# Deformable sampling on one Trainium2 core: one broad weighting per tap, half the transposes, and a corner multiplied on GpSimd

## The chip, the cores and the metric

The kernel runs on one core of one Trainium2 chip, as one program. The metric is the device time of one execution in microseconds. Five engines of the core appear below: PE (TensorE: matmuls and transposes; its weight loads are listed as PEld), DVE (VectorE), ACT (ScalarE), POOL (GpSimd, which also issues the indirect transfers) and SP (SyncE, which issues plain transfers). SBUF is the large on-chip memory, PSUM the small one into which PE writes. All engines run their own instructions in order and wait for each other by semaphores.

## The reference

Two layers of a network over x of shape (2, 128, 64, 64). The part that matters is the first mixer: four branches of deformable convolutions with kernels of 1, 1, 3 and 7, so 1 + 1 + 9 + 49 = 60 taps in all. For each tap and each of the 4096 pixels of an image, a position (py, px) is computed, the image is sampled there bilinearly, and the sample, times a mask, goes into a product with the tap's weights:

```python
def bilinear_sample(x, py, px):
    y0 = jnp.floor(py)
    x0 = jnp.floor(px)
    ...
    return v00 * (1 - wy) * (1 - wx) + v01 * (1 - wy) * wx + v10 * wy * (1 - wx) + v11 * wy * wx

def deform_conv(x, off_w, off_b, mod_w, mod_b, reg_w, k, pad):
    ...
    sampled = bilinear_sample(x, py, px) * mask[:, None]
    return jnp.einsum('bckhw,ock->bohw', sampled, reg_w.reshape(O, C, k * k))
```

v00 to v11 are the four corners around the position. After that come group norms and a fusing 1x1 convolution, a mixture of 8 experts, then the second layer with a depthwise convolution, a state-space scan and a second mixture of experts. The change touches only the weighting of the four corners and what carries it to the product.

## The kernel before, in words

**The table.** For each batch a table in HBM holds, for each pixel position, one row with the 128 channels of all four corners (4 x 128 float32 values, 2 KB). Sampling 128 pixels at one tap is therefore one indirect transfer, which fetches 128 rows into 128 partitions.

**Tiles and loops.** A batch has 4096 pixels in 8 groups (NG) of 512, a group is GT = 4 tiles of 128 pixels. `sample` runs over the 60 taps of one group; `run` calls it for the 8 groups of batch 0, then of batch 1: 2 x 8 x 60 = 960 taps. One tap does this:

- POOL issues four gathers (line 711), one for each tile, into a buffer `v` of [128 pixels, 4 tiles, 4 corners, 128 channels]. The pool of `v` has six buffers (line 610). A gather needs the indices `idx` of the group, and a buffer that the tap six before has been read out of.
- DVE weights the corners. The weights `w4` are copied to PSUM every 30 taps as `pw` (line 723). Line 740 multiplies corners 0 and 1 of all four tiles in place (1024 elements for each partition). For each half of the tiles, line 745 multiplies corners 2 and 3 into a PSUM buffer `low` (512 elements), and line 746 adds `low` onto corners 0 and 1. Two partial sums for each tile are left in `v`.
- PE transposes these to [128 channels, 512 pixels] in PSUM (line 750, tile `pst`): eight transposes, where the second of a pair accumulates onto the first and so makes the last sum.
- ACT copies `pst` to SBUF as `st` (line 759).
- Two taps later, `product` (line 779) has PE multiply `st` with the tap's weights `regw` and accumulate it in `out`, in two halves of 128 output channels. At the end of a branch ACT copies `out` to `ys` and it goes to HBM.

**What runs in between.** The order on every engine is written out by hand (a manual schedule: instructions stay in the order in which the Python code issues them). At the end of each tap, `conv.step()` issues a piece of the offset convolution, which computes indices and weights of later groups (`offset_stream`, lines 351 to 417: small matmuls on PE in line 402, window copies on ACT, position arithmetic on DVE), and `rest.step()` two or three pieces of other work: in batch 0 the normalisation of batch 1 and constant matrices, in batch 1 the end of the mixer for batch 0, its experts (lines 917 to 1009, with the product of line 991 on DVE) and the convolutions of the second layer. The group's indices come from `new_group` tiles that the offset stream fills (batch 0) or from HBM by `load_group`, a group ahead (batch 1).

Of the kernel before, what the change touches and what calls it, by code (L numbers as in the profile page):

```python
# [10 lines left out]
F32 = mybir.dt.float32  # L11
I32 = mybir.dt.int32
AF = mybir.ActivationFunctionType
ALU = mybir.AluOpType
AX = mybir.AxisListType
PSUM = bass.MemoryType.PSUM
# [3 lines left out]
P = 128  # L20
B = 2
C = 128
# [3 lines left out]
GT = 4  # L26
# [7 lines left out]
NTAP = len(TAPS)  # L34
FIRST = [0, 1, 2, 11]
NO = 3 * NTAP
TW = H + 3
E0 = 8
E1 = 64
HID = 512  # L40
DS = 16
# [67 lines left out]
def transpose4(nc, ident, ps, srcs):  # L109
    for j, s in enumerate(srcs):  # L110
        nc.tensor.transpose(ps[:, j, :], s, ident)  # L111
# [73 lines left out]
class L0Conv:  # L185
# [416 lines left out]
    def run(self, build, after):  # L602

        env, tc, nc = self.env, self.env.tc, self.env.nc
        pools = lambda ctx: lambda name, bufs, **kw: ctx.enter_context(tc.tile_pool(name=name, bufs=bufs, **kw))
        with ExitStack() as ctx:
            pool = pools(ctx)
            self.rp, self.regw = pool("l0rw", 1), {}
            self.ip = pool("l0i", 2)
            self.vp = pool("l0v", 6)  # L610
            self.stp = pool("l0s", 2)
            self.pending = []
            first = ctx.enter_context(ExitStack())
            self.open_offsets(pools(first))
            for i in range(2):
                nc.vector.memset(self.padc[i], 0.0)
            psum = ctx.enter_context(ExitStack())
            right = lambda name: pools(psum)(name, 1, space=PSUM, side="right")
            self.p_f = deque([right("l0po")])
            cur = self.new_group(self.ip)  # L620
            with (
                tc.tile_pool(name="nrm", bufs=3) as sp,
                tc.tile_pool(name="nrmp", bufs=4, space=PSUM) as pp,
            ):
                xs = []
                for g in range(NG):
                    if g % GT == 0:
                        x = self.vp.tile([P, GT, 4 * C], F32, name="v")
                    xs.append(x[:, g % GT, :])
                    nc.sync.dma_start(out=xs[g], in_=env.d["x"][0, :, g * 512 : (g + 1) * 512])  # L630
                xn = self.vp.tile([P, GT, 4 * C], F32, name="v")
                self.load_weights()
                for _ in self.zero_table(0):
                    pass
                own = lambda g: xn[:, g % GT, :].rearrange("p (j c) -> p j c", c=C)
                norms = [self.norm_group(0, g, sp, pp, "nrm", x, own(g)) for g, x in enumerate(xs)]
                together(norms[:2], 2)

                stage = self.rows(0, 0)
                self.sum_weights()  # L640
                others = Side()
                others.add(mixed(norms[2:], 3))
                for _ in range(24):
                    others.step()
                offsets = self.offset_stream([(0, 0, cur)], stage)
                while others.todo:
                    next(offsets)
                    for _ in range(3):
                        others.step()
                self.load_chunk(0)  # L650
                for _ in self.norm_end(0):
                    pass
                for _ in offsets:
                    pass
            self.p_w = pool("l0pw", 1, space=PSUM)
            self.p_r = pool("l0pr", 1, space=PSUM)
            self.p_t = pool("l0pt", 2, space=PSUM)
            self.p_o = pool("l0py", 2, space=PSUM)
            self.pending = [(n, functools.partial(self.load_chunk, c)) for n, c in ((1, 1), (3, 2))]
            early = psum.enter_context(ExitStack())  # L660
            p_m = pools(early)("l0pm", 1, space=PSUM, side="right")

            def more():

                early.close()
                self.p_f.append(right("l0po2"))
                yield


            conv, rest = Side(), Side()  # L670
            self.late, self.made = deque(), [0, 0]
            rest.add(self.norm(1, p_m, "misc"), more(), build)
            ahead = {}

            def runs():
                for g in range(1, NG):
                    ahead[g] = self.new_group(self.ip)
                    yield 0, g, ahead[g]
                    yield 1, g - 1, None
                yield 1, NG - 1, None  # L680

            conv.add(self.offset_stream(runs()))
            for g in range(NG):
                self.sample(0, g, *cur, conv, rest, 2 if g else 3)
                cur = ahead.get(g + 1)
            conv.drain()
            rest.drain()
            psum.close()
            first.close()
            side = ctx.enter_context(tc.tile_pool(name="l0ps", bufs=2, space=PSUM))  # L690
            rest.add(after(0, side))
            cur = self.load_group(1, 0)
            for g in range(NG):
                nxt = self.load_group(1, g + 1) if g + 1 < NG else None
                self.sample(1, g, *cur, conv, rest, 2)
                cur = nxt
            for f in self.late:
                f()
            for _, f in self.pending:
                f()  # L700
            self.pending = []
            rest.drain()

    def sample(self, b, g, idx, w4, conv, rest, pace):

        env, nc = self.env, self.env.nc
        pw, vs = None, {}

        def gather(v, t, tiles):
            for j in tiles:  # L710
                nc.gpsimd.indirect_dma_start(  # L711
                    out=v[:, j, :],
                    out_offset=None,
                    in_=self.table[b],
                    in_offset=bass.IndirectOffsetOnAxis(ap=idx[:, j, t : t + 1], axis=0),
                )

        for br, (k, _) in enumerate(BRANCH):
            for t in range(FIRST[br], FIRST[br] + k * k):
                tw = t % HT  # L720
                if tw == 0:
                    pw = self.p_w.tile([P, GT, HT, 4], F32, name="pw")
                    nc.vector.tensor_copy(pw, w4[:, :, t : t + HT, :])

                if b == 0 and g == 0 and t == 0:
                    for i in range(6):
                        vs[i] = self.vp.tile([P, GT, 4 * C], F32, name="v")
                        gather(vs[i], i, range(0, 2))
                if t in vs:
                    v = vs.pop(t)  # L730
                    gather(v, t, range(2, GT))
                else:
                    v = self.vp.tile([P, GT, 4 * C], F32, name="v")
                    gather(v, t, range(GT))
                v4 = v.rearrange("p j (q c) -> p j q c", q=4)


                up = v4[:, :, 0:2, :]
                w = pw[:, :, tw, 0:2].unsqueeze(3).to_broadcast([P, GT, 2, C])
                nc.vector.tensor_tensor(up, up, w, ALU.mult)  # L740
                for j in range(0, GT, 2):
                    two = slice(j, j + 2)
                    low = self.p_r.tile([P, 2, 2, C], F32, name="low")
                    w = pw[:, two, tw, 2:4].unsqueeze(3).to_broadcast([P, 2, 2, C])
                    nc.vector.tensor_tensor(low, v4[:, two, 2:4, :], w, ALU.mult)  # L745
                    nc.vector.tensor_tensor(up[:, two], up[:, two], low, ALU.add)  # L746
                pt = self.p_t.tile([P, GT, P], F32, name="pst")
                for j in range(GT):
                    for q in range(2):
                        nc.tensor.matmul(  # L750
                            pt[:, j, :],
                            v4[:, j, q, :],
                            env.ident,
                            is_transpose=True,
                            start=j == 0 and q == 0,
                            stop=j == GT - 1 and q == 1,
                        )
                st = self.stp.tile([P, 512], F32, name="st", bufs=3)
                nc.scalar.copy(st, pt.rearrange("p j t -> p (j t)"))  # L759
                self.late.append(functools.partial(self.product, b, g, br, t, st))  # L760
# [799 lines left out]
class L1Ffn:  # L1560
# [8 lines left out]
    def fetch(self, pool):  # L1569

        c = len(self.w1)
        w1 = pool.tile([P, EC, HID], F32, name="wt")
        src = self.env.d["weight1"][c * EC : (c + 1) * EC, 0:C, :].rearrange("e p h -> p e h")
        self.env.nc.sync.dma_start(out=w1, in_=src)
        self.w1.append(w1)
# [329 lines left out]
```

## Time and profile before

| what | value |
|---|---|
| median of 3 runs | 7961.13 us (7953.55 to 7967.98) |
| the profiled execution's own time | 7970.23 us |
| its span, first to last instruction | 7968.4 us |
| mean granted TensorE clock | 0.832 |
| busy over the span | PE 5681.7 us (71%), DVE 5782.8 (73%), POOL 4612.1 (58%), ACT 1988.5 (25%) |
| first gather issued, last one | 108.1 us, 5808.9 us |
| 128 to 2935 us: eight groups of batch 0 | 5.8 to 5.9 us a tap for most groups |
| 2935 to 5817 us: eight groups of batch 1 | 5.5 to 6.3 us a tap |
| the rest, from 5820 us on | 2148 us |

In the rows of the profile, "L711 POOL DMA_INDIRECT v<-table,idx x3840 | 3650.0, 951 | 2123.6 <-issue" reads: line 711 on POOL, an indirect transfer that writes `v` from `table` and `idx`, 3840 times; busy for 3650.0 us, 951 ns each; the engine stood idle for 2123.6 us just before such instructions, and the most of it ended with what is named behind the arrow ("issue": nothing that the profile shows; "remote": an event that it can't place). For a gather, the busy time on POOL is the issuing of its descriptors, not the transfer. In lists in order of time the columns are the start in us, the duration in us, then engine, line and operation, and in brackets the idle time before it.

### The profile page before, as it was taken

How to read it: one execution, taken by the hardware profiler on the slowest of the kernel's cores; microseconds unless marked ns; L12 is line 12 of the kernel's file. 1: busy time of each engine (PE TensorE's matmuls, PEld its weight loads, DVE VectorE, ACT ScalarE, POOL GpSimd, SP SyncE). 2: the span in 40 equal slices, each digit the busy share in tenths (PEclk: the TensorE clock that was granted, in tenths of full speed). 3: DMA queues.
4: the chain of work that ended last, by engine and by line, in shares of the span. 5: the costliest groups of instructions: out<-in, count | busy, mean ns of one | idle time of the engine just before them, and what ended most of it. 6: DMA issues, size and time to landing. Idle time of an engine off the chain costs nothing. (4 is left out here: it accounts for less than half of the span.)

```text
span 7968.4 us, 77973 instructions
## 1 busy us (share of the span) xinstructions
PE 5681.7 (71%) x25153; PEld 3608.9 (45%) x25153; DVE 5782.8 (73%) x8700; ACT 1988.5 (25%) x3838; POOL 4612.1 (58%) x4589
## 2 busy tenths in 40 slices
PE   4677777777777767767766878765555678756668
PEld 3455555555555534434444656543333456512124
DVE  5877777777777777678787666676756575789982
ACT  1111111111111113211111222211154255455540
POOL 3666666666666666666666666566643334357640
PEclk8888888888888878878888888887787778877789
DMA  7886767677676777877777877777654334434444
GB/s 221 254 270 210 220 206 220 211 215 219 207 221 205 217 226 256 275 237 248 229 239 211 228 208 219 217 217 229 203 163 146 116 99 134 115 128 147 148 136 148
DMA packets 645247, 1597.35 MB, mean 200 GB/s; under 512 B 168020, under 2 KB 253180, under 8 KB 640876
## 3 DMA queue, kind: packets, MB, share of 16 engines
q0 software_dynamic: 307200, 1006.88, 41.6%
q1 hardware_dynamic: 306156, 537.52, 21.4%
q10 hardware_dynamic: 31488, 47.97, 1.7%
q8 instruction: 205, 3.36, 0.2%
q14 instruction: 198, 1.62, 0.1%
HBM read 1478.65 MB, written 115.83 MB: 200 GB/s over the span
## 5 line engine op out<-in xcount | busy, mean ns | idle before, releaser
L711 POOL DMA_INDIRECT v<-table,idx x3840 | 3650.0, 951 | 2123.6 <-issue 1003.8
L779 PE MATMUL out<-st,regw 128*128 128x512 f32 x3840 | 2142.1, 685 | 131.2 <-issue 79.9
L750 PE MATMUL pst<-ident,v 128*128 128x128 f32 x7680 | 1264.9, 306 | 1072.0 <-issue 662.4
L740 DVE TENSOR_TENSOR v<-v,pw 128x1024 f32<-128x1024 f32 x960 | 1168.3, 1217 | 704.2 <-DMA v<-table,idx 566.9
L750 PEld LDWEIGHTS pst<-ident,v 128*128 128x128 f32 x7680 | 1011.9, 158 | 1455.6 <-issue 985.2
L759 ACT COPY st<-pst 128x512 f32<-128x512 f32 x960 | 557.3, 585 | 4350.9 <-remote 2356.1
L746 DVE TENSOR_TENSOR v<-v,low 128x512 f32<-128x512 f32 x1920 | 1318.1, 687 | 68.0 <-remote 1.5
L745 DVE TENSOR_TENSOR low<-v,pw 128x512 f32<-128x512 f32 x1920 | 1328.7, 692 | 33.4
L1426 POOL TENSOR_TENSOR db<-du,bcb 128x512 f32<-128x512 f32 x512 | 657.3, 1289 | 835.4 <-DVE da L1477 683.7
L779 PEld LDWEIGHTS out<-st,regw 128*128 128x128 f32 x3840 | 771.5, 223 | 747.7 <-issue 684.4
L1449 PE MATMUL py<-sc,ident 128*128 128x512 f32 x1024 | 660.6, 751 | 233.0 <-DVE sc L1487 233.0
L1477 DVE TENSOR_TENSOR_SCAN da<-da,state,db 128x512 f32<-128x512 f32 x512 | 657.0, 1283 | 177.9 <-ACT da L1433 134.4
L1449 PEld LDWEIGHTS py<-sc,ident 128*128 128x128 f32 x1024 | 200.2, 229 | 529.3 <-DVE sc L1487 436.2
L402 PEld LDWEIGHTS po<-wa,win 128*128 128x128 f32 x2112 | 330.2, 202 | 141.8 <-issue 141.2
L1152 PEld LDWEIGHTS ps<-ipw,hs 128*120 128x120 f32 x2816 | 343.3, 199 | 109.1 <-issue 75.4
L1487 DVE TENSOR_TENSOR sc<-da,bcb 128x512 f32<-128x512 f32 x512 | 354.2, 692 | 44.8 <-DVE da L1477 1.8
L402 PE MATMUL po<-wa,win 128*128 128x147 f32 x2112 | 358.3, 299 | 35.2 <-issue 34.2
L1152 PE MATMUL ps<-ipw,hs 128*120 128x64 f32 x2816 | 340.8, 281 | 45.3 <-issue 30.8
L1433 ACT ACTIVATE da<-delta,w_A_log 128x512 f32<-128x512 f32 x512 | 354.0, 692 | 18.8 <-DVE delta L1389 2.8
L1160 PEld LDWEIGHTS ps<-tm,X 120*88 120x88 f32 x2048 | 188.7, 170 | 83.7 <-ACT Y L1114 53.3
L1160 PE MATMUL ps<-tm,X 120*88 120x48 f32 x2048 | 195.6, 267 | 41.9 <-ACT Y L1114 37.9
L855 PE MATMUL pfo<-yc,fw 128*128 128x256 f32 x512 | 146.9, 423 | 80.4 <-ACT yc L857 67.3
(296 smaller groups left out, 4695.2 us busy)
## 6 DMA issues: line engine op xcount, KB each, us to landing
bcb<-bc SPq DMA_DIRECT2D x256, 512.0 KB
regw<-in_regw SPq DMA_DIRECT2D x192, 640.0 KB
v<-table,idx POOLq DMA_INDIRECT x3840
yd<-ys ACTq DMA_DIRECT2D x128, 256.0 KB
yc<-yd SPq DMA_DIRECT2D x32, 1024.0 KB
gb<-gd SPq DMA_DIRECT2D x16, 2048.0 KB
wt<-in_weight SPq DMA_DIRECT2D x32, 1024.0 KB
tm<-pos SPq DMA_DIRECT2D x16, 1440.0 KB
```

The source lines that it names most:

```text
L402: m()
L711: nc.gpsimd.indirect_dma_start(out=v[:, j, :], out_offset=None, in_=self.table[b], in_offset=bass.IndirectOffsetOnAxis(ap=idx[:, j, t : t ...
L740: nc.vector.tensor_tensor(up, up, w, ALU.mult)
L745: nc.vector.tensor_tensor(low, v4[:, two, 2:4, :], w, ALU.mult)
L746: nc.vector.tensor_tensor(up[:, two], up[:, two], low, ALU.add)
L750: nc.tensor.matmul(pt[:, j, :], v4[:, j, q, :], env.ident, is_transpose=True, start=j == 0 and q == 0, stop=j == GT - 1 and q == 1,)
L759: nc.scalar.copy(st, pt.rearrange("p j t -> p (j t)"))
L779: nc.tensor.matmul(self.out[half], self.regw[t // CH][:, t % CH, half * P : (half + 1) * P], st, start=first, stop=last,)
L1152: nc.tensor.matmul(ps[:, k, :], patch, own, start=True, stop=True)
L1426: nc.gpsimd.tensor_tensor(dbs[u], pieces[k]["du"][:, half, :], bcb[u // 2][:, 0, :], ALU.mult)
L1449: nc.tensor.matmul(py[k, half], by, what, start=first, stop=last)
L1477: nc.vector.tensor_tensor_scan(s, s, dbs.pop(u), state[:, half, n : n + 1], ALU.mult, ALU.add)
```

## The change

It replaces the five DVE operations of a tap by three, and the eight transposes by four. One multiplication weights all four corners in place (2048 elements), one add puts corners 2 and 3 onto 0 and 1 (1024 elements, both operands in SBUF), one adds corner 1 onto corner 0 (512 elements, both in SBUF). PE then transposes the single sum of each tile; the PSUM buffer `low` is gone.

In every second tap (EVERY = 2; the odd ones) DVE's multiplication covers only corners 0 to 2 (1536 elements), and corner 3 is multiplied on POOL (512 elements, with the weights from `w4` in SBUF). POOL runs in order, so that its multiplication of a tap doesn't stand ahead of the next tap's gathers, gathers are issued one tap ahead: in the iteration of tap t those of tap t+1 come first and then the multiplication of tap t. Buffers that have been asked for are kept in `held`. At the last tap of a group the first gathers of the next group are issued, with the indices that `after()` returns. In the very first group the first two tiles of six taps are gathered first, as before.

```diff
+EVERY = 2
...
-            self.p_r = pool("l0pr", 1, space=PSUM)
...
+        def fetch(idx, t):
+            if t in vs:
+                v = vs.pop(t)
+                self.gather(b, v, idx, t, range(2, GT))
+            else:
+                v = new()
+                self.gather(b, v, idx, t, range(GT))
+            return v
...
+        if not self.held:
+            self.held.append(fetch(idx, 0))
...
+                if t + 1 < NTAP:
+                    self.held.append(fetch(idx, t + 1))
+                elif after():
+                    self.held.append(fetch(after()[0], 0))
+                v = self.held.popleft()
                 v4 = v.rearrange("p j (q c) -> p j q c", q=4)
-
-
+                side = t % EVERY == EVERY - 1
+                if side:
+                    w = w4[:, :, t, 3:4].to_broadcast([P, GT, C])
+                    nc.gpsimd.tensor_tensor(v4[:, :, 3, :], v4[:, :, 3, :], w, ALU.mult)
+                n = 3 if side else 4
+                w = pw[:, :, tw, 0:n].unsqueeze(3).to_broadcast([P, GT, n, C])
+                nc.vector.tensor_tensor(v4[:, :, 0:n, :], v4[:, :, 0:n, :], w, ALU.mult)
                 up = v4[:, :, 0:2, :]
-                w = pw[:, :, tw, 0:2].unsqueeze(3).to_broadcast([P, GT, 2, C])
-                nc.vector.tensor_tensor(up, up, w, ALU.mult)
-                for j in range(0, GT, 2):
-                    two = slice(j, j + 2)
-                    low = self.p_r.tile([P, 2, 2, C], F32, name="low")
-                    w = pw[:, two, tw, 2:4].unsqueeze(3).to_broadcast([P, 2, 2, C])
-                    nc.vector.tensor_tensor(low, v4[:, two, 2:4, :], w, ALU.mult)
-                    nc.vector.tensor_tensor(up[:, two], up[:, two], low, ALU.add)
+                nc.vector.tensor_tensor(up, up, v4[:, :, 2:4, :], ALU.add)
+                nc.vector.tensor_tensor(v4[:, :, 0, :], v4[:, :, 0, :], v4[:, :, 1, :], ALU.add)
                 pt = self.p_t.tile([P, GT, P], F32, name="pst")
-                for j in range(GT):
-                    for q in range(2):
-                        nc.tensor.matmul(
-                            pt[:, j, :],
-                            v4[:, j, q, :],
-                            env.ident,
-                            is_transpose=True,
-                            start=j == 0 and q == 0,
-                            stop=j == GT - 1 and q == 1,
-                        )
+                transpose4(nc, env.ident, pt, [v4[:, j, 0, :] for j in range(GT)])
```

`gather` and the loop that issues a tap's four transfers move from a local function to a method and are otherwise the same; `transpose4` (lines 109 to 111) is one transpose for each of the four tiles.

More of the change, by code (lines that the diff above doesn't have):

```diff
@@ L611, in run @@
             self.stp = pool("l0s", 2)
-            self.pending = []
+            self.pending, self.held = [], deque()
             first = ctx.enter_context(ExitStack())
@@ L683, in run @@
             for g in range(NG):
-                self.sample(0, g, *cur, conv, rest, 2 if g else 3)
+                self.sample(0, g, *cur, conv, rest, 2 if g else 3, lambda: ahead.get(g + 1))
                 cur = ahead.get(g + 1)
@@ L694, in run @@
                 nxt = self.load_group(1, g + 1) if g + 1 < NG else None
-                self.sample(1, g, *cur, conv, rest, 2)
+                self.sample(1, g, *cur, conv, rest, 2, lambda: nxt)
                 cur = nxt
@@ L702, in run, with gather, sample @@
             rest.drain()
-    def sample(self, b, g, idx, w4, conv, rest, pace):
+    def gather(self, b, v, idx, t, tiles):
+        for j in tiles:
+            self.env.nc.gpsimd.indirect_dma_start(
+                out=v[:, j, :],
+                out_offset=None,
+                in_=self.table[b],
+                in_offset=bass.IndirectOffsetOnAxis(ap=idx[:, j, t : t + 1], axis=0),
+            )
+    def sample(self, b, g, idx, w4, conv, rest, pace, after):
         env, nc = self.env, self.env.nc
         pw, vs = None, {}
[L709 to L715, printed above, removed]
-                )
+        new = lambda: self.vp.tile([P, GT, 4 * C], F32, name="v")
+        def fetch(idx, t):
[6 more added lines that the diff above has]
+            return v
+        if b == 0 and g == 0:
+            for i in range(6):
+                vs[i] = new()
+                self.gather(b, vs[i], idx, i, range(0, 2))
+        if not self.held:
+            self.held.append(fetch(idx, 0))
         for br, (k, _) in enumerate(BRANCH):
@@ L723, in sample @@
                     nc.vector.tensor_copy(pw, w4[:, :, t : t + HT, :])
[L725 to L734, printed above, removed]
@@ L747, in sample @@
-                pt = self.p_t.tile([P, GT, P], F32, name="pst")
-                for j in range(GT):
-                    for q in range(2):
-                        nc.tensor.matmul(
-                            pt[:, j, :],
-                            v4[:, j, q, :],
-                            env.ident,
-                            is_transpose=True,
-                            start=j == 0 and q == 0,
-                            stop=j == GT - 1 and q == 1,
-                        )
+                if t + 1 < NTAP:
+                    self.held.append(fetch(idx, t + 1))
+                elif after():
+                    self.held.append(fetch(after()[0], 0))
```

## The prediction

> **What bounds the kernel now.** I read the page first, for shares and rows; then the windows, to see where the changed loop lies; then the gathers in order of time; then the neighbours of one long gather.
>
> ```profile
> span 7968.4 us, 77973 instructions
> ...
> L711 POOL DMA_INDIRECT v<-table,idx x3840 | 3650.0, 951 | 2123.6 <-issue 1003.8
> L779 PE MATMUL out<-st,regw 128*128 128x512 f32 x3840 | 2142.1, 685 | 131.2 <-issue 79.9
> L750 PE MATMUL pst<-ident,v 128*128 128x128 f32 x7680 | 1264.9, 306 | 1072.0 <-issue 662.4
> L740 DVE TENSOR_TENSOR v<-v,pw 128x1024 f32<-128x1024 f32 x960 | 1168.3, 1217 | 704.2 <-DMA v<-table,idx 566.9
> ...
> L746 DVE TENSOR_TENSOR v<-v,low 128x512 f32<-128x512 f32 x1920 | 1318.1, 687 | 68.0 <-remote 1.5
> L745 DVE TENSOR_TENSOR low<-v,pw 128x512 f32<-128x512 f32 x1920 | 1328.7, 692 | 33.4
> L1426 POOL TENSOR_TENSOR db<-du,bcb 128x512 f32<-128x512 f32 x512 | 657.3, 1289 | 835.4 <-DVE da L1477 683.7
> ```
>
> The counts give one tap: four gathers on GpSimd (POOL), five VectorE (DVE) operations, eight transposes and four matmuls on PE, and 960 taps. By the windows they all lie between 108 and 5820 us:
>
> ```profile
> 108.00:5820.00 5712.00, 4155.12 (x19101) 2756.11 (x19100) 4247.68 (x6529) 995.15 (x1918) 3649.97 (x3840) 0.85 0.73 226
> ```
>
> The columns are PE, PE's weight loads, DVE, ACT and POOL busy, then clock, DMA share, GB/s. No engine looks full: POOL 64%, DVE 74%, PE 73%. But POOL's 64% counts only the 0.95 us of each gather. In order of time, POOL alone:
>
> ```profile
> 1064.15 0.94 POOL L711 DMA_INDIRECT v<-table,idx  x1 [2.87 <-remote]
> 1065.40 0.95 POOL L711 DMA_INDIRECT v<-table,idx  x1 [0.30 <-issue]
> ...
> 1077.91 0.95 POOL L711 DMA_INDIRECT v<-table,idx  x1 [0.30 <-issue]
> 1081.62 0.94 POOL L711 DMA_INDIRECT v<-table,idx  x1 [2.76 <-remote]
> ```
>
> A gather follows the last after 0.30 us, so each costs 1.25 us and a tap 5.0 us: 3840 × 1.25 = 4800 us of the 5709 us from the first gather to the last add. Every third tap or so POOL stops for 2 to 3 us, always before the first gather of a tap. Over all gaps longer than 0.5 us, what is above 0.30 us comes to 883 us. 4800 + 883 + 30 us of lengthened gathers is the stage. At those stops POOL wants the buffer of six taps before, and PE is late in reading it:
>
> ```profile
> 2022.79 1.04 PE L750 MATMUL pst<-ident,v 128*128 128x128 f32 x8
> 2028.27 0.27 PE L750 MATMUL pst<-ident,v 128*128 128x128 f32 x1 [1.09 <-issue]
> 2028.97 0.47 PE L750 MATMUL pst<-ident,v 128*128 128x128 f32 x1 [0.44 <-DMA v<-table,idx]
> ```
>
> Eight transposes usually take 1.04 us; here they crawl, 0.7 us apart, and POOL resumes at 2030.76. So the stage is POOL's issue pace, 5.0 us a tap, plus 0.92 us in which it waits for PE. DVE follows: 566.9 us of its idle time is waiting for gathers, typically 2.9 us after the last of a tap has been issued.
>
> **What the change costs, part by part.** Only this stage is touched.
>
> DVE: out go 1217 + 2 × 692 + 2 × 687 = 3975 ns a tap. From 512 to 1024 elements 525 to 530 ns are added, so 1536 elements cost about 1.75 us and 2048 about 2.28 us. With the adds of 1024 (1.22 us) and 512 (0.69 us) a tap is 4.19 us, or 3.66 us where POOL has a corner: mean 3.92 us, 0.05 us less. DVE's whole load stays near 4.4 us a tap (4248/960 now), below POOL's pace. On the end: nothing.
>
> PE: four transposes fewer, 0.52 us a tap (half of 1.04). ACT's copy stays.
>
> POOL, multiplication: 480 of 128x512, 1289 ns each by L1426. The gap beside a gather isn't in the trace: nothing between two such multiplications, 0.30 us between two gathers; I take the middle, 1.44 us. 480 × 1.44 = 691 us, ends 619 and 763. It goes on POOL's own queue between the gathers of tap t+1 and t+2, so those gathers stand behind it, and behind them DVE. It waits for the data of tap t; that was issued one tap ahead, and the 5.0 us of tap t+1's gathers cover the 2.9 us of landing. Without that cover it would cost 480 × 2.9 = 1390 us.
>
> POOL, gathers beside DVE's adds: this is the term that decides. Until now no DVE operation of a tap reads two operands from SBUF: pw and low lie in PSUM. Both new adds do. The expert stage has such an operation, L991, beside gathers:
>
> ```profile
> 3587.55 1.23 DVE L991 TENSOR_TENSOR gb<-gb,xnt 128x1024 f32<-128x1024 f32 x1 [7.39 <-DMA gb<-gd]
> 3587.72 1.87 POOL L711 DMA_INDIRECT v<-table,idx  x1 [0.30 <-issue]
> ...
> 3592.39 0.94 POOL L711 DMA_INDIRECT v<-table,idx  x1 [0.30 <-issue]
> 3592.60 1.22 DVE L991 TENSOR_TENSOR gb<-gb,xnt 128x1024 f32<-128x1024 f32 x1
> ...
> 3603.83 2.35 DVE L991 TENSOR_TENSOR gb<-gb,xnt 128x1024 f32<-128x1024 f32 x2
> 3605.00 2.00 POOL L711 DMA_INDIRECT v<-table,idx  x1 [0.30 <-issue]
> ```
>
> A gather that begins inside the operation is held until the operation ends and finishes 0.82 us later (3587.72: 1.87 us instead of 0.95); one that begins just before it (3592.39) is not touched. Beside L745 and L746 no lengthening shows. Over these L991 the excess is 8.6 us, 0.27 us for each. A tap brings 1.22 + 0.69 us of such adds, so by length 0.27 + 0.15 = 0.42 us: 403 us in all, the lower end. L991 came where POOL often stood at a like phase. If starts 1.25 us apart fall evenly, the longer add catches one 88% of the time for a mean 0.55 us (0.48) and the shorter 46% for 0.28 us (0.13): 0.61 us, 586 us, which I take. The upper end, each add holding a gather for its length less 0.12 us, is 1.67 us, 1603 us.
>
> The other direction: beside L989, a POOL multiplication of 4.5 us, L991 is up to 5.5 us long. So an add can stand behind a multiplication for up to 1.29 us, 0.65 us a tap at most; DVE's 4.4 + 0.65 = 5.05 us is still below POOL's 6.3 us. Hidden.
>
> Here a rule of the Trainium skill can be weighed. The row is the gather of 1.87 us beside L991. The page "SBUF — State Buffer", section "Who interferes with whom", says that a VectorE operation with two SBUF inputs contends only with GpSimd instructions that read SBUF, and infers that writing a gather's descriptors isn't stopped by a tensor_tensor. By that inference the gathers would keep 1.25 us and the sum below would lose 586 us, ending near 7830; by the row it keeps them. The row decides.
>
> POOL's waits for PE: 883 us now; the ends are 0 and 883. At 5.0 + 0.72 + 0.61 = 6.3 us, three taps take 19 us instead of 17.5, while PE does 1.6 us less in them; its busy time was 16.3 us of 17.5 in the two periods around 2030, so some 4 us come free, about the length of a crawl, and six buffers ride over the rest. I keep a tenth, 90 us.
>
> Two smaller things. Each tap's gathers are issued one iteration earlier in program order, across a group's end too; POOL only waits there for indices that are ready some twenty taps before in batch 0 and loaded a group ahead in batch 1: nothing. And the PSUM buffer low goes: nothing.
>
> Sum: 4800 + 691 + 586 + 90 = 6167 us, and the 30 us of today's lengthening stays: 6197. Before: 5709. That is +488 on the profiled execution's own 7970.2 us: 8458; the median of the runs shown is 9 us lower, so 8449. The phase of adds and gathers is not free: after a multiplication the add and the next gather start within about 0.1 us of each other, and if the gather is first it escapes, so I take some 50 us off the gather term, to 537 us: **8400 us**.
>
> **Rivals.** A, faster: the gathers slip past. POOL's order is fixed, and the phase may lock so that most start just before an add, as at 3592.39. For it: 12 of 38 gathers beside L991 were lengthened. Against: two adds in a row last 1.91 us and starts are 1.25 us apart, so one must begin inside. With 0.1 us a tap: 4800 + 691 + 96 + 90 + 30 = 5707; with none, 5611. On the median that is 7959 and 7863. It decides when held gathers and PE waits together cost under 5709 − 4800 − 691 − 30 = 188 us, 0.2 us a tap. I put the case at 7863.
>
> B, all in the gaps, hardly slower: POOL's additions fill its idle 883 us at their lower ends: 4800 + 619 + 403 + 30 = 5852, +143, 8104. For it: the measured 0.27 us. It is the lower end of my forecast.
>
> C, much slower: PE's crawls don't overlap with POOL's longer tap and the 883 us stay: 6197 + 793 = 6990, +1281, 9242. For it: the crawls hardly depend on transposes. Against: six buffers at a slower pace.
>
> **How the numbers follow.** Forecast with B: 0.82, A: 0.12, C: 0.06. The forecast's own range runs from B to an even-phase gather cost half as large again (+290): 8100 to 8700. A and C together hold 0.18 and stay mostly outside; I go a little below B for a cheaper gather, to 8030. About 0.2% (16 us) is what can be told from no change: a thin strip at A's upper edge, 0.02. Faster 0.11, same 0.02, slower 0.87.
>
> **What would show it.** After: gathers' mean from 951 ns to 1.08 to 1.11 us, the long ones beginning inside an add; POOL's multiplication near 1.3 us; DVE's rows at about 2.28, 1.75, 1.22 and 0.69 us; 3840 transposes; POOL's waits on PE far below 883 us; a tap of 6.3 us. I am wrong if the gathers stay at 0.95 us (A), if POOL still stops each third tap (C), or if POOL's multiplications wait for landings.

## The result, and the profile after

| what | before | after |
|---|---|---|
| median of 4 runs each | 7957.34 us (7940.24 to 7967.98) | 8292.67 us (8272.18 to 8305.77) |
| the profiled execution's own time | 7970.23 us | 8305.77 us |
| first gather issued to last add | 5708.6 us | 6029.5 us |
| the rest of the profiled execution's time | 2262 us | 2276 us |

The changed kernel is slower: the ratio is 1.0429, with a 95% interval from 1.0412 to 1.0447. Of the 335.5 us between the two profiled executions, 321 us lie in the stage of the gathers.

Page of the changed kernel, its span and the groups that answer to those shown of before:

```profile
span 8303.8 us, 69331 instructions
...
L706 POOL DMA_INDIRECT v<-table,idx x3840 | 4304.2, 1121 | 1178.3 <-issue 906.0
...
L112 PE MATMUL pst<-ident,v 128*128 128x128 f32 x3840 | 755.0, 331 | 1925.6 <-issue 1786.7
...
L754 DVE TENSOR_TENSOR v<-v 128x1024 f32<-128x1024 f32 x960 | 1180.1, 1229 | 596.7 <-POOL v L749 461.4
...
L755 DVE TENSOR_TENSOR v<-v 128x512 f32<-128x512 f32 x960 | 668.6, 696 | 33.0
L749 POOL TENSOR_TENSOR v<-v,w 128x512 f32<-128x512 f32 x480 | 511.0, 1065 | 102.8 <-DMA v<-table,idx 82.9
```

The same kernel, groups by form: DVE's multiplication in its two widths.

```profile
L752 DVE TENSOR_TENSOR v<-v,pw 128x2048 f32<-128x2048 f32 x480 | 1095.8, 2283 | 220.2 <-DMA v<-table,idx 184.6 <-PE pst L112 22.4 <-issue 6.2
L752 DVE TENSOR_TENSOR v<-v,pw 128x1536 f32<-128x1536 f32 x480 | 841.3, 1753 | 797.1 <-DMA v<-table,idx 666.0 <-issue 65.6 <-PE pst L112 38.7
```

And the stage by the windows (columns as before: PE, its weight loads, DVE, ACT, POOL, clock, DMA share, GB/s):

```profile
108.00:6148.00 6040.00, 3933.27 (x15258) 2374.48 (x15256) 4313.34 (x4611) 1011.96 (x1920) 4813.99 (x4319) 0.82 0.71 213
```

Three things are to be seen. The gathers went from 951 to 1121 ns each, 654 us more over 3840 of them. POOL's own multiplication took 1065 ns, not 1289. And POOL's busy time in the stage rose from 3650 to 4814 us while the stage grew by only 321 us: something that POOL did before, waiting, is gone. The gap list of POOL says what. Before, 421 gathers had a gap of more than 0.5 us ahead of them; after, 9 have. E5 to E7 take up why. The rows of DVE are those that were forecast.

Since POOL's chain sets the stage, it can be added up term by term: 3840 gathers at 0.95 + 0.30 us; what gathers took beyond an undisturbed one (0.944 us, so that the sums hold to within some 4 us); the multiplications with what they change in the gaps around them; and POOL's waits. The two columns on the right are the same two kernels in another batch of runs, told below (E5 and E6).

| POOL's chain, us | before | after | before again (E6) | after again (E5) |
|---|---|---|---|---|
| 3840 gathers × 1.25 | 4800 | 4800 | 4800 | 4800 |
| gathers lengthened | 30 | 675 | 29 | 664 |
| 480 multiplications | 0 | 453 | 0 | 453 |
| POOL's waits | 883 | 102 | 116 | 84 |
| sum | 5713 | 6030 | 4945 | 6001 |
| first gather to last add, measured | 5708.6 | 6029.5 | 4941.6 | 5993.9 |

The multiplication's 453 us are 511 us of busy time less 58: there is a gap of 0.02 us before it and of 0.16 us after it, where two gathers have one of 0.30 us (480 × 0.12 = 58).

Where the 675 us arise is seen in order of time (start, duration, engine, operation, idle time before it), the changed kernel:

```profile
2011.89 0.95 POOL L706 DMA_INDIRECT v<-table,idx  x1 [0.30 <-issue]
2012.86 1.05 POOL L749 TENSOR_TENSOR v<-v,w 128x512 f32<-128x512 f32 x1
2013.94 1.23 DVE L754 TENSOR_TENSOR v<-v 128x1024 f32<-128x1024 f32 x1 [1.68 <-POOL v L749]
2014.07 1.97 POOL L706 DMA_INDIRECT v<-table,idx  x1 [0.16 <-POOL v L749]
2015.20 0.69 DVE L755 TENSOR_TENSOR v<-v 128x512 f32<-128x512 f32 x1
...
2016.34 0.95 POOL L706 DMA_INDIRECT v<-table,idx  x1 [0.30 <-issue]
```

POOL's multiplication ends at 2013.91. DVE has stood waiting for it and starts the add 0.03 us later; POOL's next gather starts 0.16 us after the same end, so it begins inside the add. The add ends at 2015.17, and the gather is done 0.87 us after that: 1.97 us in place of 0.95. That is not a chance meeting. In 363 of 479 cases the add starts right behind the multiplication like this, and in those the gather behind it lasts 1.96 us in the mean; in the others 1.08 us. Of the 957 gathers that took over 1.0 us, 855 began inside the add of 1024 (L754), none beside DVE's multiplication (L752, of 1497 that began there).

### The profile page after: what moved, and what is told of

Its sections match the earlier page's. It is cut to its first block, busy times and chain, and to the rows that moved or that the text cites. A ratio compares the mean times of both kernels' runs of the same rounds, so it can differ in the third digit from the quotient of the medians.

```text
span 8303.8 us, 69331 instructions
## 1 busy us (share of the span) xinstructions
PE 5465.4 (66%) x21313; PEld 3234.4 (39%) x21313; DVE 5843.9 (70%) x6780; ACT 2004.9 (24%) x3838; POOL 5778.9 (70%) x5069
## 5 line engine op out<-in xcount | busy, mean ns | idle before, releaser
L706 POOL DMA_INDIRECT v<-table,idx x3840 | 4304.2, 1121 | 1178.3 <-issue 906.0
L752 DVE TENSOR_TENSOR v<-v,pw 128x2048 f32<-128x2048 f32 x960 | 1937.0, 2018 | 1017.3 <-DMA v<-table,idx 850.7
L779 PE MATMUL out<-st,regw 128*128 128x512 f32 x3840 | 2408.5, 762 | 75.0 <-ACT ys L793 75.0
L112 PE MATMUL pst<-ident,v 128*128 128x128 f32 x3840 | 755.0, 331 | 1925.6 <-issue 1786.7
L754 DVE TENSOR_TENSOR v<-v 128x1024 f32<-128x1024 f32 x960 | 1180.1, 1229 | 596.7 <-POOL v L749 461.4
L112 PEld LDWEIGHTS pst<-ident,v 128*128 128x128 f32 x3840 | 519.4, 168 | 2370.9 <-issue 2223.4
L1426 POOL TENSOR_TENSOR db<-du,bcb 128x512 f32<-128x512 f32 x512 | 657.6, 1290 | 852.9 <-DVE da L1477 696.0
L779 PEld LDWEIGHTS out<-st,regw 128*128 128x128 f32 x3840 | 858.6, 247 | 756.1 <-issue 659.3
L755 DVE TENSOR_TENSOR v<-v 128x512 f32<-128x512 f32 x960 | 668.6, 696 | 33.0
L749 POOL TENSOR_TENSOR v<-v,w 128x512 f32<-128x512 f32 x480 | 511.0, 1065 | 102.8 <-DMA v<-table,idx 82.9
L1152 PE MATMUL ps<-ipw,hs 128*120 128x64 f32 x2816 | 323.9, 274 | 26.6 <-ACT X L1114 15.0
```

Of the source, the lines that this page charges most:

```text
L706: self.env.nc.gpsimd.indirect_dma_start(out=v[:, j, :], out_offset=None, in_=self.table[b], in_offset=bass.IndirectOffsetOnAxis(ap=idx[:, ...
L752: nc.vector.tensor_tensor(v4[:, :, 0:n, :], v4[:, :, 0:n, :], w, ALU.mult)
L754: nc.vector.tensor_tensor(up, up, v4[:, :, 2:4, :], ALU.add)
L755: nc.vector.tensor_tensor(v4[:, :, 0, :], v4[:, :, 0, :], v4[:, :, 1, :], ALU.add)
L779: nc.tensor.matmul(self.out[half], self.regw[t // CH][:, t % CH, half * P : (half + 1) * P], st, start=first, stop=last,)
L1152: nc.tensor.matmul(ps[:, k, :], patch, own, start=True, stop=True)
```

## The experiments

Kernels that ran together share their runs of before. There were four such batches, and before itself took 7195, 7197, 7988 and 7215 us in them, where it took 7957 in the first result. Each ratio below is to before of the same batch. What is behind that difference is taken up with E5 to E7.

**E1: the change without POOL's multiplication.** DVE weights all four corners in every tap.

```diff
-                side = t % EVERY == EVERY - 1
+                side = False
```

> The changed kernel without POOL's multiplication: DVE weights all four corners in every tap; gathers stay one tap ahead, the two adds and the four transposes stay. My theory (POOL's queue alone sets the pace: 5.0 us of gathers a tap, what the adds hold them, and POOL's own multiplication): the stage loses the 511 us of multiplications less 58 us of saved gaps, and the 92 us that POOL waited for data at them, so 6030 - 545 = 5485 us, 5.7 us a tap, and the kernel ends near 7750 us, faster than the kernel before; gathers keep a mean near 1.12 us. Rival (PE paces the stage as before, or DVE does with 4.2 us of corners and 0.5 us of other work): no more than half of that is gained, 8000 us or above.

Measured: 7582.17 us, 168 us below the expectation. The ratio to before, 1.0535 [1.0512, 1.0558], is to a before of 7195 us. By form:

```profile
L706 POOL DMA_INDIRECT v<-table,idx x3840 | 4104.5, 1069 | 1286.9 <-issue 992.7 <-DMA v<-table,idx 108.6 <-DMA table<-zero 71.8
```

The multiplication's 453 us are gone, and with them 194 us of the lengthening, which the forecast didn't tie to it: gathers of 1069 ns, 481 us in all. Waits are 45 us. A pace of 5.47 to 5.68 us a tap. So with the multiplication gathers lose more beside the adds, though it runs on the same engine as they do; E9 and E11 show how.

**E2: the adds read one operand from PSUM.** Their second operand is a zero tile there, so the sum over the corners is left out; widths and order stay. The first add no longer reads POOL's product, so it doesn't wait for POOL either.

```diff
+            self.z = self.p_r.tile([P, GT, C], F32, name="z")
...
-                nc.vector.tensor_tensor(up, up, v4[:, :, 2:4, :], ALU.add)
-                nc.vector.tensor_tensor(v4[:, :, 0, :], v4[:, :, 0, :], v4[:, :, 1, :], ALU.add)
+                nc.vector.tensor_tensor(up, up, self.z.unsqueeze(2).to_broadcast([P, GT, 2, C]), ALU.add)
+                nc.vector.tensor_tensor(v4[:, :, 0, :], v4[:, :, 0, :], self.z, ALU.add)
```

> The changed kernel with POOL's multiplication, but both adds take their second operand from a PSUM tile of zeros, so sizes and order stay and no add reads two operands from SBUF; the sum over the corners is left out. My theory (adds with two SBUF operands hold the gathers): the gathers fall back to a mean of 0.95 us, the 675 us of lengthening go, and the kernel ends near 7620 us, if PE's waits don't come back, and up to 7750 us if 100 us or so of them do. Rival (POOL's new place in the order, its multiplication or its waiting for data costs the time): gathers shorten little and the kernel stays above 8100 us.

Measured: 7667.28 us, ratio 1.0654 [1.0624, 1.0684]. From the page:

```profile
L709 POOL DMA_INDIRECT v<-table,idx x3840 | 3681.5, 959 | 1176.5 <-issue 812.6
```

959 ns a gather: 59 us of lengthening in place of 675, 30 of which before had as well. The adds take as long as ever (1221 and 686 ns). That the adds don't wait for POOL here isn't the reason: 724 gathers still began inside the add of 1024 and 462 inside that of 512, and they took 953 and 963 ns in the mean, none over 1.0 us. So it isn't DVE's being busy that holds a gather, and not the add's width: it is the second operand in SBUF. Against the changed kernel that is 625 us less (other batch), of which the lengthening explains 616.

Two operands in SBUF are not the only case, though. Of 29 gathers that began inside L567 of the changed kernel, a TENSOR_SCALAR with one tensor operand, 20 took over 1.0 us; the lengthening is 0.08 us in the mean there.

The Trainium skill's page "SBUF — State Buffer", section "Who interferes with whom", says that a VectorE instruction with two SBUF inputs contends with a GpSimd instruction that reads SBUF, and infers that a tensor_tensor doesn't stop GpSimd from writing a gather's descriptors. The inference doesn't hold here: 675 us of lengthening with two operands in SBUF, 59 us with one. The rule on reads may, since a gather also takes its indices from the tile `idx`; no run separates the two.

**E3 and E4: the order alone, and the order with POOL's multiplication.** E3 has the changed kernel's issue order (`fetch`, `held`) around before's five DVE operations and eight transposes. E4 adds to E3 the multiplication of corner 3 on POOL in every second tap, so that this corner is weighted twice there:

```diff
+                if t % EVERY == EVERY - 1:
+                    w = w4[:, :, t, 3:4].to_broadcast([P, GT, C])
+                    nc.gpsimd.tensor_tensor(v4[:, :, 3, :], v4[:, :, 3, :], w, ALU.mult)
```

> The kernel before with nothing but the new order: gathers one tap ahead in the program; five DVE operations, eight transposes, no multiplication on POOL. My theory: the order costs nothing, 7957 us within 30 us. Rival (the order itself is part of the loss: one of six buffers is taken by the tap ahead): 8050 us or more.

> The same as the order alone, plus POOL's multiplication of corner 3 in every second tap, which is then weighted twice; DVE still does its five operations with low in PSUM. My theory: the 453 us that POOL's multiplications add fill the 883 us in which POOL waited for PE, since no add holds a gather; time within 60 us of the kernel before, waits for PE down to about 430 us. Rival (additive): 453 us more, near 8410 us.

Measured: E3 7208.56 us, ratio 1.0014 [1.0001, 1.0027]; E4 7670.88 us, ratio 1.0659 [1.063, 1.0688]. The order costs 14 us (by the interval 1 to 19 us). The expectation for E4, that waits for PE would absorb the multiplication, was a miss, because in this batch there were hardly any (E3's gaps hold 121 us). In place of that E4 gives the price of the multiplication beside DVE operations that hold no gather: 7670.88 − 7208.56 = 462 us, 0.96 us each, beside the 453 us that the changed kernel's own trace adds up to.

**E5 to E7: both kernels again, and before with four transposes.** E3's before of 7195 us raised a new question: 7957 or 7195? E5 is the changed kernel and E6 before, both unedited, and in E7 before transposes only the first partial sum of each tile, so that corners 1 and 3 are left out of the product:

```diff
-                for j in range(GT):
-                    for q in range(2):
-                        nc.tensor.matmul(
-                            pt[:, j, :],
...
+                transpose4(nc, env.ident, pt, [v4[:, j, 0, :] for j in range(GT)])
```

> The changed kernel itself once more. On the chip of the first four experiments the kernel before took 7195 us and not 7957. My theory (the changed kernel is bound by POOL's queue alone, and what differs between the chips is only the time that POOL of the kernel before waited for PE): the changed kernel takes the same 8290 us within 40 us wherever it runs, so the loss is 335 us where the kernel before takes 7957 and about 1095 us, a ratio of 1.15, where it takes 7195. Rival (that chip is faster at everything): the ratio stays at 1.04, that is about 7500 us.

> The kernel before, for its profile on the chip of this batch. My theory: where it takes 7195 us, POOL's waits for PE are near 120 us instead of 883 us and the transposes of a tap don't crawl; where it takes 7957 us they do both. Rival: the gathers themselves or the landing of their data are faster there.

> The kernel before with only the first of a pair of partial sums transposed: four transposes, no other change, no further add; corners 1 and 3 are left out of the product. My theory: four transposes fewer let PE keep up, so POOL's waits for PE go: where the kernel before takes 7957 us this ends at 7200 to 7350 us; where it takes 7195 us there is nothing left to win, 7150 to 7210 us. Rival (PE's crawls don't depend on the number of transposes): above 7700 us on the slower chip.

Measured: E5 8258.07 us, ratio 1.1485 [1.1454, 1.1516], in the batch with before at 7197. E6's page:

```profile
span 7212.5 us, 77973 instructions
...
L711 POOL DMA_INDIRECT v<-table,idx x3840 | 3648.2, 950 | 1357.4 <-issue 915.2
```

The same instructions and the same 950 ns a gather as in the profile of before, but POOL's idle time is 766 us less (1357.4 for 2123.6), and the mean clock is 0.881 for 0.832. Gaps over 0.5 us are 64 here and 421 there, and hold 116 us for 883. The transposes don't crawl: those of one tap take 2.57 us at the longest, where in the first profile of before they take over 3 us in 72 of 960 taps, and up to 8.88 us. So before has a time with PE's stops (7957 us, and most likely 7988 us, in whose batch E10 shows them) and one without (7195, 7197 and 7215 us). The changed kernel, at 6.1 to 6.46 us a tap, has nearly the same time in both batches (8293 and 8258 us). That is not because POOL hides the stops. They aren't there. A usual set of transposes in the changed kernel, four back to back:

```profile
2022.34 0.60 PE L112 MATMUL pst<-ident,v 128*128 128x128 f32 x4
```

In both profiles of the changed kernel the four transposes of a tap take 1.12 us at the longest. Of the kernels that ran with before at 7988 us, E10 has 27 taps over 3 us, E9 and E11 have none. In the two batches with stops, before and E10 take 5.9 us a tap, stops included, and the kernels that show none 6.1 us or more; why a slower pace should go without them isn't shown. A low clock alone doesn't bring them: both profiles of the changed kernel ran at a mean of 0.81 without them, the first profile of before at 0.83 with them.

What the change costs therefore depends on what it is compared with: 335 us in the first result, 1061 us here. The table above shows it: the added terms are the same (1098 and 1088 us), and only what they can eat up differs (883 or 116 us of waits).

E7: 7181.9 us, ratio 0.9985 [0.9968, 1.0002]: with no stops there, half the transposes win nothing. E12, the same kernel in a later batch, was meant to meet a before with stops:

> The kernel before with four transposes and nothing else, once more, in the hope of a chip on which the kernel before takes some 7960 us (corners 1 and 3 are left out of the product). My theory after the kernel with three adds, where POOL still lost 584 us on such a chip, now about every 16 gathers instead of 12: PE comes to a stop after a like number of its own instructions, so four transposes put the stops further apart and don't remove them: 7600 to 7800 us, POOL's waits 500 to 700 us. Rival (the transposes' time is what PE lacked): 7350 us or less, waits under 250 us. Where the kernel before takes 7195 us: 7180 us again, which tells nothing new.

It met one of 7215 us and gave 7207.26 us, ratio 0.9978 [0.9962, 0.9995], which says nothing on the stops. What makes PE stop, and why only in some batches, stays open. The batch with before at 7988 us and the one with 7215 us carry the same chip number, so that number alone doesn't tell them apart.

**E8: a smaller edit.** Before's multiplications with `low` in PSUM stay; one add of 512 with both operands in SBUF makes the last sum, and four transposes are left.

```diff
+                nc.vector.tensor_tensor(v4[:, :, 0, :], v4[:, :, 0, :], v4[:, :, 1, :], ALU.add)
...
+                transpose4(nc, env.ident, pt, [v4[:, j, 0, :] for j in range(GT)])
```

> The kernel before with one more add on DVE (512 elements, both operands in SBUF, 0.69 us) and four transposes; low stays in PSUM, no multiplication on POOL, gathers in the order of before. My theory: that add holds gathers for 0.15 to 0.25 us a tap, and DVE with 4.66 us of corners and 0.5 us of other work, 5.15 us a tap, comes level with POOL, 5.2 us: about 5.3 us a tap, 7350 us on either chip. Rival (an add of 0.69 us passes between the gathers and costs nothing): 7200 us or less where the kernel before takes 7195 us.

Measured: 7453.67 us, ratio 1.0357 [1.0337, 1.0378]; the expectation was 100 us too low. The lengthening is 131 us, 102 us above that of before (E6): 0.11 us a tap, where an even phase gives 0.13 for such an add. POOL's waits are 268 us, 193 of them for PE's reading of `pst`: with five DVE operations and an add, DVE is busy for 4880 us of the stage, 5.08 us a tap, about POOL's own 5.0 + 0.14 us. That PE reads the buffer later because of it is likely, not shown.

**E9: the add, but not right behind POOL's multiplication.** In the taps where POOL has a corner, DVE first copies one column of POOL's product, so that it waits for POOL ahead of its own multiplication and not between that and the add:

```diff
+            self.dot = self.stp.tile([P, 1], F32, name="dot", bufs=1)
...
                     nc.gpsimd.tensor_tensor(v4[:, :, 3, :], v4[:, :, 3, :], w, ALU.mult)
+                    nc.vector.tensor_copy(self.dot, v4[:, 0, 3, 0:1])
```

> The changed kernel, where DVE in every second tap first copies one column of POOL's product to a scratch tile and only then multiplies corners 0 to 2: the same work, but DVE's first add starts 1.8 us after POOL's multiplication ends instead of at once. In the profile of the changed kernel the add starts 0.03 us after it in 363 of 479 cases and the next gather 0.16 us after it, and that gather lasts 1.97 us. My theory (what decides is which of the two starts first when both are let go by the same multiplication): those 363 x 1.02 = 370 us go, 100 to 200 us of them come back where the moved adds meet other gathers, and the kernel ends at 8020 to 8190 us. Rival (the lengths of the adds alone set what is held): 8258 us within 40 us or, as DVE starts later, more.

Measured: 8098.14 us, ratio 1.0136 [1.0096, 1.0177] to a before of 7988 us; 160 to 195 us below the changed kernel's two medians, with 480 operations more. The same stretch in order of time:

```profile
2011.12 1.06 POOL L750 TENSOR_TENSOR v<-v,w 128x512 f32<-128x512 f32 x1
...
2012.34 1.05 POOL L707 DMA_INDIRECT v<-table,idx  x1 [0.16 <-POOL v L750]
2012.48 0.15 DVE L751 COPY dot<-v 128x1 f32<-128x1 f32 x1
...
2012.53 1.74 DVE L754 TENSOR_TENSOR v<-v,pw 128x1536 f32<-128x1536 f32 x1
...
2013.70 0.95 POOL L707 DMA_INDIRECT v<-table,idx  x1 [0.30 <-issue]
...
2014.30 1.23 DVE L756 TENSOR_TENSOR v<-v 128x1024 f32<-128x1024 f32 x1
...
2014.95 1.40 POOL L707 DMA_INDIRECT v<-table,idx  x1 [0.30 <-issue]
```

What DVE starts behind POOL's multiplication now is the short copy and then a multiplication that reads its weights from PSUM, and the gather at 2012.34 is done in 1.05 us, not 1.97. The add comes later and meets the third gather 0.65 us after its own start: 0.45 us lost. Mean excess of a gather, by its place behind the multiplication:

| gather behind POOL's multiplication | 1st | 2nd | 3rd | 4th | 5th | 6th | 7th | 8th |
|---|---|---|---|---|---|---|---|---|
| changed kernel, us | 0.805 | 0.075 | 0.026 | 0.245 | 0.143 | 0.069 | 0.025 | 0.014 |
| E9, us | 0.075 | | 0.370 | | | 0.366 | | |

In the changed kernel the first alone carries 480 × 0.805 = 386 of the 675 us. E9 lost 177 and 174 us at the third and sixth, 484 in all. So what the meeting at the release costs is 180 to 191 us of lengthening (664 or 675 less 484), in line with the 160 to 195 us of time; E1, with no release at all, had 481.

**E10: three adds of 512 and no multiplication on POOL.** Shorter adds should catch fewer gathers for less time each.

```diff
-                side = t % EVERY == EVERY - 1
+                side = False
...
-                nc.vector.tensor_tensor(up, up, v4[:, :, 2:4, :], ALU.add)
+                for q in range(2):
+                    nc.vector.tensor_tensor(v4[:, :, q, :], v4[:, :, q, :], v4[:, :, 2 + q, :], ALU.add)
```

> The changed kernel without POOL's multiplication (7582 us, gathers lengthened by 481 us), with the first add in two halves: three adds of 512 elements, 0.69 us each, in place of 1.22 and 0.69 us. My theory (a gather that starts inside an add waits for that add's end, and starts that fall between two adds pass): by even phase 3 x 0.13 = 0.39 us a tap, 375 us, so the lengthening falls by about 100 us and the kernel ends near 7480 us. Rival (the total time of such adds counts, 2.06 us against 1.91 us): 520 us of lengthening, 7620 us.

Measured: 7935.42 us, ratio 0.9943 [0.9923, 0.9963] to a before of 7988 us. The time was missed by 455 us, the lengthening was not: 292 us, less than expected, for E1's 481. The rest are stops of PE, which this batch has. POOL alone, in order of time:

```profile
2513.06 1.23 POOL L706 DMA_INDIRECT v<-table,idx  x1 [0.30 <-issue]
2517.64 1.15 POOL L706 DMA_INDIRECT v<-table,idx  x1 [3.35 <-remote]
...
2537.27 0.95 POOL L706 DMA_INDIRECT v<-table,idx  x1 [0.30 <-issue]
2540.91 0.94 POOL L706 DMA_INDIRECT v<-table,idx  x1 [2.69 <-remote]
```

3.35 and 2.69 us are what before showed every 12 gathers or so; here they come every 16 or so, 584 us over the stage. This is the one version with the whole sum that beat before, and only in a batch where before most likely has stops: 0.6%. Against a before without them its lengthening alone should make it slower; that wasn't run.

**E11: POOL's multiplication in every tap** (`EVERY = 1`).

> The changed kernel with EVERY = 1: POOL multiplies corner 3 in every tap. My theory (POOL's queue alone): 480 more multiplications at 0.94 us net (451 us), and their first gathers held 0.8 us instead of the 0.25 us of a tap without one (some 250 us): 8900 to 9000 us, gathers' mean near 1.19 us. Rival (DVE, with 0.5 us less a tap, gives something back or the holds don't follow the multiplications): 8700 us or less.

Measured: 8973.87 us, ratio 1.1238 [1.1184, 1.1292]. The page's row for the gathers, and for the add of 1024 what ended the idle time before it (us, times):

```profile
L706 POOL DMA_INDIRECT v<-table,idx x3840 | 4599.0, 1198 | 1102.6 <-issue 695.6
```

```profile
  POOL v L749: 2219.2, 881
```

In 881 of 960 taps the add waited for POOL, and so started together with the gather behind the multiplication: 94% of those gathers were long, by 0.954 us in the mean. That is 913 us of a lengthening of 970, for 386 of 675 with half as many multiplications. The effect grows with the number of releases, which speaks for the release and against the adds' mere length: those are the same in both kernels.

## Why the prediction was right

**What bounds the kernel.** POOL's chain of 1.25 us a gather was the right place, and the sum of its terms closes to within 7 us on every kernel of the table. What one profile could not show is that 883 us of waits for PE belong to some batches alone. The forecast holds for the comparison it was made for, and its +439 us is 622 short of the loss of 1061 us against the before of 7197, though the changed kernel's own time was the same there.

**Multiplication on POOL: mis-sized.** Forecast 691 us, the trace adds up to 453, E4 gives 462. The row that it was priced by, L1426 with 1289 ns, reads two full operands; here one is four values, broadcast, and it took 1065 ns. That the broadcast makes the difference wasn't tested by itself. And the gap that I set at 0.15 us, as "the middle" between nothing and 0.30, is 0.02 before and 0.16 after in place of 0.30, so it takes 0.12 off and adds nothing.

**Gathers beside the adds: right in kind, a little small.** 537 + 30 = 567 us forecast, 675 measured; E2 shows that the operand in SBUF does it, as read off L991. The step that failed is the shading: "after a multiplication the add and the next gather start within about 0.1 us of each other, and if the gather is first it escapes". The 0.1 us is right (0.16 − 0.03 = 0.13), but where both are let go by the multiplication, in 363 of 479 cases, the add wins by those 0.13 us each time. The gather was first in 105 of the others, where DVE came later, and 89 of these escaped. The 50 us taken off should have been put on. Without POOL's multiplication, E1's 481 us lie between the low end by length, 403 + 30, and the even phase, 586 + 30, and nearer to the former. The time that the prediction gives by the page's inference, 7830 us, doesn't follow from its sum: 8449 − 586 = 7863.

**POOL's waits: right in size, of another kind.** 90 us forecast, 102 measured, but not a leftover of the waits for PE. 93 of the 102 us are at the multiplication, 82 of these waiting for gathered data (31 cases), which the prediction had covered by the 5.0 us of the next tap's gathers. Before a gather 9 us are left. Rival C, that PE's crawls would stay, fell: 9 long gaps for 421. But the prediction had six buffers ride over crawls that go on, and in the changed kernel's profile there are none: a tap's transposes take 1.12 us at most, for 8.88 us before. So this term came out right for a reason that it didn't give. What took the crawls away stays open; four transposes alone didn't, since E10 has four as well.

**The order in `held`: nothing**, and E3 measured 14 us. **PE's 0.52 us a tap: off the path**, and E7 and E12 found nothing to win by it, in batches without stops. **DVE: nothing**, with rows of 2283, 1753, 1229 and 696 ns for 2.28, 1.75, 1.22 and 0.69 us; its waits for POOL, 461 us or 0.48 us a tap, stayed below the 0.65 us allowed and hidden.

**Rivals.** A, gathers that slip past the adds, needed under 0.2 us a tap; they lost 0.67. B, the low end at 8104, had the multiplication at 619 and the gathers at 403: the one was still too dear, the other far too cheap. That the 8293 us came out within 110 us of the forecast is partly luck: two errors, +238 us and −108 us, went against each other; the waits (−12) and the 14 us outside the stage are small beside them.

## What to carry to other kernels

Where GpSimd issues indirect gathers one behind the other, a VectorE operation with both operands in SBUF wasn't free here (675 us), however idle VectorE looked: keep one operand in PSUM (59 us), or make such operations short. And before an engine hands a result to another in the middle of such a chain, ask what both start when it is done: if the consumer's next operation blocks the producer's next instruction, they can meet nearly every time (94% in E11), not by chance; move the wait ahead of some harmless operation. Before a gain is read as "so many us of waits can be filled", look at a second run of the kernel before on its own: a wait that isn't always there can't always be filled.

## What the runs showed of the hardware that was not expected

- Released by the same GpSimd multiplication, VectorE's operation starts 0.03 us after its end and GpSimd's own next gather 0.16 us after. Those 0.13 us are what makes the gather lose.
- GpSimd's multiplication of 128x512 took 1.06 us with a broadcast operand in every run that had it, and 1.29 us with two full ones (L1426).
- The same kernel before took 7195 to 7215 us in three batches and 7957 to 7988 us in two, with gathers of 950 and 951 ns in the two that were profiled: the difference is stops of PE, 116 us of POOL's waits or 883. Their cause wasn't found. The changed kernel shows no such stops in either batch.
